# Two-step normalising at the start, att copies in older bursts, and one v product between two score tiles: a change to a group-norm attention kernel

## The chip, the cores and the metric

The kernel runs on one core of a Trainium2 chip. The metric is device time in microseconds: from the first to the last instruction of the core and what lies around them, as the median of several executions. The profile is of one further execution and lists every instruction with its engine, start and duration.

## What is computed

The input x has 4 batches of 512 channels by 48 x 48 pixels (T = 2304 positions). A batch is group-normalised (32 groups of 16 channels), projected to q, k and v, put through attention with 8 heads of 64 channels, projected again and added to x:

```
hn = _group_norm(x, gn_scale, gn_bias)
qkv = einsum('oc,bchw->bohw', qkv_w, hn) + qkv_b
q, k, v = (fp16, per head, d = 64)
w = softmax(einsum('bhct,bhcs->bhts', q * scale, k * scale), axis=-1)
a = einsum('bhts,bhcs->bhct', w, v).astype(float32)
out = einsum('oc,bchw->bohw', proj_w, a) + proj_b
return x + out
```

## The kernel before

The 512 channels lie in 4 chunks of 128 partitions (NC = 4), the 2304 positions in 5 blocks (NQ = 5): four of 512 columns and a last one, block 4, of 256. Heads are treated two at a time, as 4 pairs for each batch, so there are 16 pairs in all. `hn[b, c, j]` is batch b, chunk c, block j of x; it is normalised in place.

**Start.** Batch 0 is normalised before anything else can run. `stats` (L621) takes the statistics of one block on VectorE (DVE), `aggregate` (L625) joins the five of a chunk. For chunk 0, `first_group` (L678 to L686) averages over groups by two tiny matmuls with a matrix of sixteenths: one of the mean, then, after DVE has computed the variance with the deviation of the means (L680), one of that; GpSimd (POOL) raises to the power -1/2 (L686); DVE makes scale `ga` and bias `gb` (L690, L691); ScalarE (ACT) then applies them to the five blocks in the order 0 to 4 (`norm_chunk`, L706). Chunks 1 to 3 go through `group_scale` (L635 to L647) and `coefficients` (L654 to L666): a 32 x 32 transpose, `bn_aggr` over the 16 channels, the power on POOL, a copy that spreads the result, a transpose back, three small operations, and ACT again. DVE fits statistics of the next chunk between these steps. TensorE (PE) keeps its clock with matmuls on a constant (`keep_busy`, L1317) until it can begin the eight projection chains of pair 0 (L748): k of blocks 0 to 4, then q of blocks 0 to 2; all eight take chunk 0, then all take chunk 1, and so on.

**Stream.** Then comes a stream of bursts written out in program order. Burst n makes three score tiles (`scores`, L998: six matmuls of 512 columns, or twelve of 256 in block 4), whose exponentials ACT takes (L1005, tile by tile into `p`); three score banks rotate, so a tile waits for the exponential of the tile three before it. Two bursts later PE multiplies `p` with v (`values`, L1023, into the one bank `av`), and DVE copies a finished `av` to `avx` (L1032) and adds up `p` (`add`, L1054, L1059) for the softmax sums. The sums of a block are made by PE (`add_up`, L1082, into the same bank as `av`), copied to `slx` by DVE (L1098), sent through DRAM by SyncE (SP) and inverted (L1127); POOL divides (`divide`, L1147) and writes `att`. For blocks 2 and 3 of the last pair (`soon`; block 4 is the stream's end) the sums come two bursts after the block's end rather than three, and for block 3 DVE inverts in place (L1108).

**Work beside the stream.** All other work is a list of pieces. `fill` takes pieces from the list in each burst, as many as a credit allows: a projection of a later pair (L748, L799), or an output projection `pr` (L887, eight matmuls of 512 columns, evacuated by DVE at L914). `fill` runs after `values`, except in a burst that closes a block's sums, where it runs before. The output projection needs `att` as 32-bit copies `a32`, which `att32` makes on ACT (L881) or on POOL (L879). In the last batch the blocks 3, 2 and 4 are projected in two goes: pairs 0 to 2 first (FIRST, six matmuls; its three copies per block are issued together at the first of the block's pieces), pair 3 last (LAST, two matmuls).

The order on every engine is the program's order; each engine works its own list from front to back.

Of the kernel before, what the change touches and what calls it, by code (L numbers as in the profile page):

```python
# [24 lines left out]
GROUP = C // 32  # L25
# [442 lines left out]
def fast_path(  # L468
# [201 lines left out]
    def first_group():  # L670

        mean, var = moments[:, 1, 0:1], moments[:, 2, 0:1]
        by = share.rearrange("p g j -> p (g j)")
        pm = small_bank("first_group")
        dev, var2, mg, veps, rstd = (
            small_tile(1, f"first_{n}") for n in ("dev", "var2", "mg", "veps", "rstd")
        )
        nc.tensor.matmul(pm[:, 0:1], by, mean, start=True, stop=True)  # L678
        nc.vector.tensor_tensor(dev, mean, pm[:, 0:1], ALU.subtract)
        nc.vector.tensor_scalar(var2, dev, dev, var, ALU.mult, ALU.add)  # L680
        nc.tensor.matmul(pm[:, 1:2], by, var2, start=True, stop=True)
        nc.vector.scalar_tensor_tensor(
            mg, pm[:, 0:1], -1.0, gsc[:, 0:1], ALU.mult, ALU.mult
        )
        nc.vector.tensor_scalar(veps, pm[:, 1:2], EPS, None, ALU.add)
        nc.gpsimd.tensor_tensor(rstd, veps, mhalf[:, 0:1], ALU.pow)  # L686

        def finish():
            ga, gb = small_tile(1, "first_ga"), small_tile(1, "first_gb")
            nc.vector.tensor_tensor(ga, rstd, gsc[:, 0:1], ALU.mult)  # L690
            nc.vector.tensor_scalar(gb, rstd, mg, gbi[:, 0:1], ALU.mult, ALU.add)  # L691
            ab[0, 0] = ga, gb

        return finish
# [5 lines left out]

    def norm_chunk(b, c):

        ga, gb = ab[b, c]
        for j in range(NQ):
            t = hn[b, c, j]
            nc.scalar.activation(t, t, AF.Identity, bias=gb, scale=ga)  # L706

# [156 lines left out]
    def att32(b, j, pairs=range(NC)):  # L867
        o, n = QBLOCKS[j]
        for c in pairs:
            if left_over(b, j):  # L870
                t = xpool.tile([P, n], F32R, tag=f"x{c}_{j}", name=f"a32_{b}_{j}_{c}")
            else:
                t = work.tile(
                    [P, QB], F32R, tag=f"a32_{c}", bufs=1, name=f"a32_{b}_{j}_{c}"
                )
            at32[b, j, c] = t[:, :n]
            source = atts[b * NPAIR + c][:, o : o + n]
            if c in beside_exps() and not (pairs == LAST and left_over(b, j)):
                nc.gpsimd.tensor_copy(at32[b, j, c], source)  # L879
            else:  # L880
                nc.scalar.copy(at32[b, j, c], source)  # L881
# [55 lines left out]
    def proj_pieces(b, j):  # L937

        def ahead(k):
            if k < len(proj_list) and not in_two(b, proj_list[k][0]):
                residual(b, *proj_list[k])

        def begin():
            att32(b, j, LAST if in_two(b, j) else range(NC))
            if j == 0:
                ahead(0)
                ahead(1)

        pairs = LAST if in_two(b, j) else range(NC)
        chains = [
            proj_piece(b, j, chunks, pairs, lambda k=k: ahead(k + 2))
            for k, (jj, chunks) in enumerate(proj_list)
            if jj == j
        ]
        return [piece(0.0, begin)], chains
# [28 lines left out]
    def scores(u):  # L986
# [5 lines left out]
        for r in range(BURST):  # L992
            ps = ps_s.tile([P, 2, QB], F32, tag="ps", name=f"ps_{g}_{j}_{k}_{r}")
# [237 lines left out]
    def put_first(b, j):  # L1231

        for jj, chunks in proj_list:
            if jj == j:
                put([proj_piece(b, j, chunks, FIRST)])

    for b in range(B):
# [20 lines left out]
        if b == B - 1:  # L1258
# [4 lines left out]

            ahead = [
# [4 lines left out]
            ]  # L1269
            for j in range(NQ):  # L1270
                put_proj(old, j, ahead)
                if j + 1 < NQ:
                    put_convert(old, j + 1)

            for j in (NQ - 2, NQ - 3, NQ - 1):
                there = ends[(NG - 2) * NQ + j] + BEHIND + 6
                put_run(att32, b, j, FIRST, after=there)
                put_first(b, j)
# [34 lines left out]
    idle = ps_av.tile([P, QB], F32, tag="av", name="idle")  # L1313

    def keep_busy(count):
# [5 lines left out]
    def all_stats(c):  # L1321
        for j in range(NQ):
            stats(0, j, c)
        aggregate(0, (c,))

    keep_busy(16)
    all_stats(0)
    first_coefficients = first_group()
    keep_busy(4)

    eight = [(1, j) for j in range(NQ)] + [(0, j) for j in range(8 - NQ)]
# [10 lines left out]
    for c in range(NC):  # L1342

        for j in range(NQ):
            if j == (1 if c < 2 else 2):
                if c == 0:
                    first_coefficients()
                else:
                    coefficients(0, (c,))
                norm_chunk(0, c)  # L1350
            if c + 1 < NC:
                stats(0, j, c + 1)
        if c + 1 < NC:
            aggregate(0, (c + 1,))
            group_scale(0, (c + 1,))
# [75 lines left out]
    for n in range(end):  # L1431
# [5 lines left out]
        scores(stream[n])  # L1437
# [6 lines left out]
        if summed:  # L1444

            fill(n)
        if n >= BEHIND:
# [9 lines left out]
        if not summed:  # L1457
# [158 lines left out]
```

## Time and profile before

| What | us |
|---|---|
| median of 3 executions | 1601.38 |
| range of the three | 1600.72 to 1603.44 |
| the profiled execution, whole | 1602.89 |
| its span, first to last instruction | 1601.2 |
| PE busy | 1583.9 (99%) |
| ACT busy | 1268.1 (79%) |
| DVE busy | 1137.0 (71%) |
| POOL busy | 327.9 (20%) |

A timeline row gives the start in us from the span's start, the us up to the end of the merged group, the engine, the line of the kernel, the operation, out<-in with partitions and shape, the count, and in brackets the idle time before it with what ended it. PE's ends are modelled, so a busy PE can hide stretches in which it only waits; starts are measured, and the distance between the starts of the same step in two neighbouring bursts is the surer measure.

### The profile page before, as it was taken

The numbers are of one execution on the slowest core, as the hardware profiler recorded it, in microseconds if no ns is written. First come the engines' busy times: TensorE is split into PE (matmuls) and PEld (weight loads), VectorE is DVE, ScalarE is ACT, GpSimd is POOL, SyncE is SP. The second block draws the span as 40 slices with busy tenths as digits, with TensorE's granted clock in tenths as the row PEclk, the third lists the DMA queues.
The fourth block names the chain that finished last, engine by engine and source line by source line (L and its number), as shares of the span: only waits on it lengthen the run. The fifth ranks groups of instructions, "written<-read, shape, count | busy, mean of one in ns | idle before, by whom it ended". The sixth has DMA issues, their size and how long they took to land.

```text
span 1601.2 us, 28364 instructions
## 1 busy us (share of the span) xinstructions
PE 1583.9 (99%) x11524; PEld 695.0 (43%) x11524; DVE 1137.0 (71%) x1298; ACT 1268.1 (79%) x1362; POOL 327.9 (20%) x460
## 2 busy tenths in 40 slices
PE   9999999999999999999999999999999999999997
PEld 3533434443333534555333354445533334435554
DVE  6177668876666678887666666888767776766775
ACT  3177777888888888888888888877878888888895
POOL 1011212222121222222112111222212121111322
PEclk9999999999999999999999999999999999999999
DMA  7002020000000024521000001353101000015424
GB/s 217 8 14 67 11 71 17 18 15 12 14 18 15 9 70 119 145 64 28 11 15 18 14 12 41 111 154 90 25 15 18 15 15 11 15 31 163 151 67 128
DMA packets 94896, 82.10 MB, mean 51 GB/s; under 512 B 50852, under 2 KB 60964, under 8 KB 94756
## 3 DMA queue, kind: packets, MB, share of 16 engines
q1 hardware_dynamic: 92724, 78.35, 18.1%
q8 instruction: 92, 1.51, 0.4%
q10 hardware_dynamic: 1904, 1.84, 0.4%
q14 instruction: 48, 0.39, 0.1%
q0 software_dynamic: 128, 0.01, 0.0%
HBM read 60.70 MB, written 19.17 MB: 50 GB/s over the span
## 4 chain that ended last, share of the span: by engine, by line
PE 96%; DVE 1%; ACT 1%; DMA 1%; POOL 0%; issue 0%; SPq 0%; DVEq 0%
PE pqk L748 29%; PE ps L998 20%; PE av L1023 20%; PE pv L799 15%; PE pr L887 8%; PE sl L1082 2%; PE ps L748 1%; ACT p L1005 1%; DMA x<-x_dram 0%; DMA r<-x_dram 0%; DVE acc L1054 0%; PE first_av L748 0%; PE first_w L748 0%; DVE st L621 0%; POOL a L879 0%
## 5 line engine op out<-in xcount | busy, mean ns | idle before, releaser
L1005 ACT ACTIVATE p<-ps 128x1024 f16<-128x1024 f32 x1296 | 1233.3, 1025 | 302.5 <-PE ps L998 299.5
L1054 DVE TENSOR_TENSOR acc<-acc,p 128x3072 f16<-128x3072 f16 x270 | 487.2, 1805 | 54.0 <-ACT p L1005 51.6
L748 PE MATMUL pqk<-x,wqkv 128*64 128x512 f32 (+1 forms) x2432 | 510.2, 549 | 0.1
L1023 PE MATMUL av<-p,v 128*64 128x512 f16 (+1 forms) x2880 | 360.8, 364 | 0.4 <-DVE slx L1098 0.3
L998 PE MATMUL ps<-q,k 64*128 64x512 f16 (+1 forms) x2880 | 356.2, 358 | 1.5 <-ACT p L1005 1.1
L799 PE MATMUL pv<-wqkv,x 128*64 128x256 f32 x2304 | 267.5, 379 | 0.0
L748 PEld LDWEIGHTS pqk<-x,wqkv 128*64 128x64 f32 x2432 | 168.0, 137 | 205.9 <-issue 156.2
L1120 POOL TENSOR_SCALAR in<-sums 128x8 f32<-128x8 f32 (+1 forms) x158 | 101.3, 641 | 723.8 <-DMA sums<-slx 717.2
L998 PEld LDWEIGHTS <-k 64*128 64x128 f16 x2880 | 106.0, 94 | 288.5 <-issue 239.6
L1023 PEld LDWEIGHTS <-v 128*64 128x64 f16 x2880 | 131.3, 109 | 213.3 <-issue 168.6
L1147 POOL TENSOR_TENSOR att<-avx,ib 128x512 f16<-128x512 f32 (+1 forms) x78 | 126.5, 1622 | 434.2 <-DMA ib<-row 372.4
L799 PEld LDWEIGHTS pv<-wqkv,x 128*64 128x64 f32 x2304 | 161.7, 137 | 85.4
L1054 DVE TENSOR_TENSOR acc<-p,p 128x3072 f16<-128x3072 f16 x79 | 138.1, 1748 | 0.0
L887 PE MATMUL pr<-a,whi 128*128 128x512 f32 (+1 forms) x311 | 121.9, 399 | 2.6 <-DVE r L914 2.2
L1059 DVE TENSOR_TENSOR acc<-acc 128x1024 f16<-128x1024 f16 x156 | 112.5, 721 | 3.3
L887 PE MATMUL pr<-a,wlo 128*128 128x512 f32 (+1 forms) x311 | 113.6, 373 | 0.0
L758 DVE TENSOR_SCALAR k<-pqk,bqkv 128x512 f16<-128x512 f32 (+1 forms) x75 | 52.1, 695 | 77.4 <-PE pqk L748 77.2
L807 DVE TENSOR_TENSOR v<-pv,bv 128x512 f16<-128x512 f32 x72 | 49.6, 689 | 80.9 <-PE pv L799 80.8
L758 DVE TENSOR_SCALAR q<-pqk,bqkv 128x512 f16<-128x512 f32 (+1 forms) x77 | 53.4, 694 | 74.6 <-PE pqk L748 74.4
L1098 DVE COPY slx<-sl 128x512 f32<-128x512 f32 (+1 forms) x79 | 50.6, 640 | 66.0 <-PE sl L1082 66.0
L914 DVE SCALAR_TENSOR_TENSOR r<-pr,bproj,r 128x512 f32<-128x512 f32 (+1 forms) x80 | 54.9, 694 | 45.3 <-PE pr L887 40.2
L1032 DVE COPY avx<-av 128x512 f32<-128x512 f32 (+1 forms) x79 | 50.6, 640 | 38.5 <-PE av L1023 38.1
(102 smaller groups left out, 498.6 us busy)
## 6 DMA issues: line engine op xcount, KB each, us to landing
r<-x_dram SPq DMA_DIRECT2D x72, 256.0 KB, 3.6
out_dram<-r SPq DMA_DIRECT2D x69, 256.0 KB, 2.7
ib<-row SPq DMA_DIRECT2D x126, 128.0 KB, 3.1
x<-x_dram SPq DMA_DIRECT2D x62, 256.0 KB, 4.1
x<-x_dram SPq DMA_DIRECT2D x16, 128.0 KB, 5.0
sums<-slx SPq DMA_DIRECT2D x128, 2.0 KB, 2.1
ib<-row SPq DMA_DIRECT2D x30, 64.0 KB, 2.9
wqkv<-qkv_wT_dram SPq DMA_DIRECT2D x2, 768.0 KB, 6.9
```

Of the source, the lines that this page charges most:

```text
L748: nc.tensor.matmul(pw[0][lo : lo + D, :n], wqkv[:, c, w0 + lo : w0 + lo + D], hn[b, c, j], start=(c == 0), stop=(c == NC - 1),)
L758: nc.vector.tensor_scalar(qk[g][part][:, o : o + n], pw[0][:, :n], bqkv[:, col : col + 1], SCALE, ALU.add, ALU.mult,)
L799: nc.tensor.matmul(pw[0][lo : lo + D, a, :], hn[b, c, i * P // QB][:, at + lo : at + lo + D], wqkv[:, c, 2 * C + half * C // 2 :][:, : C / ...
L887: nc.tensor.matmul(ps[:, :n], w[:, c, bass.ts(m, P)], at32[b, j, c], start=(i == 0), stop=(i == len(steps) - 1),)
L914: nc.vector.scalar_tensor_tensor(xt[:, i], places[i], bias, xt[:, i], ALU.add, ALU.add)
L998: nc.tensor.matmul(ps[:, h, a * n : (a + 1) * n], kt[rows, bass.ts(i, P)], qt[rows, o : o + n], start=True, stop=True,)
L1005: nc.scalar.activation(pt[:, r], ps, AF.Exp)
L1023: nc.tensor.matmul(av[0][lo : lo + D, :n], vv[b, pr // 2][:, i, pr % 2 * P + lo : pr % 2 * P + lo + D], pt[:, r, h, a * n : (a + 1) * n], ...
L1054: nc.vector.tensor_tensor(t, before, pt, ALU.add)
L1059: nc.vector.tensor_tensor(t[:, 0], t[:, 0], t[:, r], ALU.add)
L1120: nc.gpsimd.tensor_scalar(t, sm, limit, None, op)
L1147: nc.gpsimd.tensor_tensor(atts[g][:, o : o + n], avx.pop((g, j))[:, :n], ibs.pop((g, j))[:, :n], ALU.mult,)
```

## The change

Three edits, each in its own place.

1. **Start.** Normalising is split in two steps where a block is needed first: ACT first applies the group-independent scale and the shift by the mean (`x * gsc + mg`, with mg = -mean * gsc), while the variance is still on its way; a second step multiplies by rstd and adds the bias. In chunk 0 block 4 and block 0 get this, block 4's second step by DVE and block 0's by ACT; in chunks 1 to 3 block 4 gets it, both steps by ACT. The variance of chunk 0's means is added by a second accumulating matmul, in a bank of its own. The eight chains now begin with k of block 4. DVE takes the statistics of chunk c + 1 before its coefficients and no longer between them; only block 0 of chunk 1 is still taken in between.
2. **Copies.** In the last batch, the copies of pairs 0 and 1 of the blocks 3, 2 and 4 are separate entries, one ahead of each of six output projections of batch 2, and remain on ACT; those of block 0 move from ACT to POOL. Pair 2's copy of block 3 goes ahead as well, and moves to POOL; those of blocks 2 and 4 are issued ahead of the first two projections of block 2. Block 2's early copies get tiles of their own that x has left (`x1_1`, `x3_1`).
3. **Near the end.** In the burst two after the end of the last pair's block 3, that block's last product with v stands between the second and third score tile. In the two bursts that follow the two `soon` sums, `fill` comes before `values`.

A listing of the two instruction orders shows besides that three projection pieces in the last batch's middle pairs move by half a chain, one burst earlier. SP's list is the same.

```
-        nc.tensor.matmul(pm[:, 0:1], by, mean, start=True, stop=True)
-        nc.vector.tensor_tensor(dev, mean, pm[:, 0:1], ALU.subtract)
-        nc.vector.tensor_scalar(var2, dev, dev, var, ALU.mult, ALU.add)
-        nc.tensor.matmul(pm[:, 1:2], by, var2, start=True, stop=True)
-        nc.vector.scalar_tensor_tensor(
-            mg, pm[:, 0:1], -1.0, gsc[:, 0:1], ALU.mult, ALU.mult
-        )
-        nc.vector.tensor_scalar(veps, pm[:, 1:2], EPS, None, ALU.add)
+        nc.tensor.matmul(pm, by, mean, start=True, stop=True)
+        nc.tensor.matmul(pv, by, var, start=True, stop=False)
+        nc.vector.tensor_tensor(dev, mean, pm, ALU.subtract)
+        nc.vector.tensor_tensor(dev2, dev, dev, ALU.mult)
+        nc.tensor.matmul(pv, by, dev2, start=False, stop=True)
+        mg = shifted(c, "a", pm)
+        small_first, then = hn[0, c, NQ - 1], hn[0, c, 0]
+        by_scalar(small_first, gsc[:, c : c + 1], mg)
+        by_scalar(then, gsc[:, c : c + 1], mg)
+        nc.vector.tensor_scalar(veps, pv, EPS, None, ALU.add)
         nc.gpsimd.tensor_tensor(rstd, veps, mhalf[:, 0:1], ALU.pow)
+        meanwhile()
+        by_vector(small_first, rstd, gbi[:, c : c + 1])
+        by_scalar(then, rstd, gbi[:, c : c + 1])
+        scale_bias(c, "a", rstd, mg)
+        for j in range(1, NQ - 1):
+            by_scalar(hn[0, c, j], *ab[0, c])
...
+    def next_group(c):
...
+        aggregate(0, (c,))
...
+        nc.vector.tensor_copy(by_group(means), to_channels(grouped[:, :, 0]))
+        nc.vector.transpose(mean_cols, means)
+        mg = shifted(c, tag, mean_cols[:, c : c + 1])
+        first = hn[0, c, NQ - 1]
+        by_scalar(first, gsc[:, c : c + 1], mg)
...
+        nc.vector.tensor_copy(by_group(scales), to_channels(rstd))
+        nc.vector.transpose(cols, scales)
+        by_scalar(first, cols[:, c : c + 1], gbi[:, c : c + 1])
+        scale_bias(c, tag, cols[:, c : c + 1], mg)
+        for j in range(NQ - 1):
+            by_scalar(hn[0, c, j], *ab[0, c])
...
-            if c in beside_exps() and not (pairs == LAST and left_over(b, j)):
+            if beside or c in beside_exps() and not (pairs == LAST and left_over(b, j)):
                 nc.gpsimd.tensor_copy(at32[b, j, c], source)
...
-            att32(b, j, LAST if in_two(b, j) else range(NC))
+            if in_two(b, j):
+                att32(b, j, LAST)
+            elif (b, j) == (B - 1, 0):
+                att32(b, j, range(len(EARLY), NC))
+            else:
+                att32(b, j)
...
         for r in range(BURST):
+            if r == BURST - 1 and ahead_of_last:
+                ahead_of_last()
...
+            ahead += [
+                (att32, b, j, (c,)) for j in (NQ - 2, NQ - 3, NQ - 1) for c in EARLY
+            ]
+            ahead.append((att32, b, NQ - 2, THIRD))
...
+            ahead = [
+                (att32, b, NQ - 3, THIRD),
+                (att32, b, NQ - 1, THIRD),
+                *((att32, b, 0, (c,), True) for c in EARLY),
+            ]
             for j in (NQ - 2, NQ - 3, NQ - 1):
-                there = ends[(NG - 2) * NQ + j] + BEHIND + 6
-                put_run(att32, b, j, FIRST, after=there)
-                put_first(b, j)
+                put_first(b, j, ahead if j != NQ - 2 else [])
...
-        scores(stream[n])
+        inside = n - BEHIND == soon[1]
+        scores(stream[n], (lambda: values(stream[n - BEHIND])) if inside else None)
...
-        if summed:
+        filled = summed or n - BEHIND - 1 in soon
+        if filled:
             fill(n)
-        if n >= BEHIND:
+        if n >= BEHIND and not inside:
             values(stream[n - BEHIND])
...
-        if not summed:
+        if not filled:
             fill(n)
```

## The prediction

> **What bounds the kernel now.** I read the busy times first, then PE's waits, then the timeline of the start and of the last 100 us, because the change touches only those.
>
> ```profile
> PE 1583.9 (99%) x11524; PEld 695.0 (43%) x11524; DVE 1137.0 (71%) x1298; ACT 1268.1 (79%) x1362; POOL 327.9 (20%) x460
> ```
>
> PE is the bound; what is not PE work can be won only where PE stands still. PE's waits, by what ended them:
>
> ```profile
> PE pr L887 <- DVE r L914: 2.2, 1, 2.2
> PE ps L748 <- ACT x L706: 1.3, 1, 1.3
> PE ps L998 <- ACT p L1005: 1.1, 3, 0.5
> PE av L1023 <- DVE slx L1098: 0.3, 1, 0.3
> PE sl L1082 <- DVE avx L1032: 0.2, 1, 0.2
> ```
>
> The first (near 1048 us, a late residual from DRAM) is not touched. The other four are what the edits can reach: the start, three waits for exponentials, one for `slx`, one for `avx`. The start, in the timeline:
>
> ```profile
> 9.07 0.38 PE L681 MATMUL first_group<-first_var,share 128*128 128x1 f32 x2 [0.56 <-DVE first_var L680]
> 9.80 0.58 POOL L686 TENSOR_TENSOR first_rstd<-first_veps,mhalf 128x1 f32<-128x1 f32 x1 [4.69 <-DVE first_veps L685]
> 10.49 0.27 DVE L691 TENSOR_SCALAR first_gb<-first_rstd,first_mg,gbi 128x1 f32<-128x1 f32 x1
> 10.80 3.42 ACT L706 ACTIVATE x<-x,first_gb,first_ga 128x512 f32<-128x512 f32 x5 [4.60 <-DVE first_gb L691]
> 11.67 4.94 PE L748 MATMUL ps<-x,wqkv 128*64 128x512 f32 x24 [1.34 <-ACT x L706]
> 18.16 4.89 PE L748 MATMUL ps<-x,wqkv 128*64 128x512 f32 x24
> ```
>
> Useful PE work starts at 11.67. A chunk takes 18.16 - 11.67 = 6.49 us and later ones 6.44 (24.60 - 18.16): a chain is 0.86 us for 512 columns, 0.43 for 256, and 7 x 0.86 + 0.43 = 6.45. So once begun PE doesn't stop, and the start is worth exactly what its first matmul gains, if it is then kept fed. The two stalls at the copies and the ones near the end, PE and ACT:
>
> ```profile
> 1512.73 1.67 ACT L881 CAST a<-att 128x512 fp32r<-128x512 f16 x3
> 1516.29 0.60 PE L998 MATMUL ps<-q,k 64*128 64x512 f16 x4
> 1517.20 0.39 PE L998 MATMUL ps<-q,k 64*128 64x512 f16 x2 [0.30 <-ACT p L1005]
> 1519.89 0.82 PE L998 MATMUL ps<-q,k 64*128 64x512 f16 x6
> 1530.45 0.39 PE L998 MATMUL ps<-q,k 64*128 64x512 f16 x2 [0.27 <-ACT p L1005]
> 1562.07 0.84 PE L1023 MATMUL av<-p,v 128*64 128x512 f16 x6 [0.35 <-DVE slx L1098]
> 1577.85 0.63 PE L998 MATMUL ps<-q,k 64*128 64x256 f16 x8
> 1579.00 0.39 PE L998 MATMUL ps<-q,k 64*128 64x256 f16 x4 [0.52 <-ACT p L1005]
> 1581.02 0.84 PE L1082 MATMUL sl<-acc,ones 128*64 128x512 f16 x6 [0.19 <-DVE avx L1032]
> 1582.43 0.83 PE L998 MATMUL ps<-q,k 64*128 64x256 f16 x12
> ```
>
> The bracket understates a stall, since a modelled end swallows part of it. Undisturbed bursts there with a six-matmul projection are 3.12 us apart by their score tiles (0.75 scores, 0.77 v product, 1.60 projection; 1523.34 to 1526.46). The burst at 1516.29 lasts 3.60, so its stall is 0.48, not 0.30; that at 1529.58 lasts 3.56 (to 1533.14): 0.44.
>
> **What the Trainium skill says.** "Perfetto Trace Analysis", section Identifying the Most-Contended Engine, says that matmul busy share is no good measure for TensorE because pipelined matmuls blur it. This trace agrees: 99% busy, with 0.48 us lost where 0.30 is shown; hence the distances. "ScalarE: Activation LUTs", Rules for kernel authors, gives about 0.3 us per activation and 0.83 ns per element: an estimate of 0.51 for 256 and 0.73 for 512; measured are 0.585 and 0.80 (0.71 from start to start), which I use. "GPSIMD Engine Reference", section 1 Specifications, has POOL share its memory interface with DVE. The trace agrees: a 512-column copy on POOL takes 0.61 alone and up to 2.23, DVE's 3072-column addition 1.75 and 2.06 to 2.12 beside POOL. It matters for the copies that go to POOL.
>
> **Edit 1, the start.** Removed from the path: the wait of the second matmul for DVE's 0.27 us variance (now a 0.15 us square: about 0.12 saved), `ga`, `gb` and the hand-over (10.38 to 10.80), and one ACT block of 512. New times: moments at 8.07; means at 8.51; dev 8.55, square 8.74 to 8.89; variance matmul 8.95 to 9.33; veps to 9.52; power on POOL 9.61 to 10.19. Meanwhile mg is ready at 9.09 and ACT shifts block 4 (9.13 to 9.71) and block 0 (to about 10.4). DVE's second step on block 4 has a like in the trace, the later `norm` of 256 columns, 0.36 us at least: 10.22 to 10.58, so PE starts at about 10.65 (a 0.07 hand-over as at 11.60 to 11.67). Its first chain lasts 0.43, to 11.08. Block 0 needs ACT's second step, 10.4 to 11.2: PE goes on at 11.25 and then has 7 x 0.86 = 6.02 to do, to 17.27 against 18.16: **0.9 us** gained; 1.05 if block 0 isn't late, 0.7 if ACT's two steps on one block follow each other 0.2 later.
>
> It must stay fed. DVE takes for a chunk about 2.75 (five statistics, four at 0.61 and one at 0.41) + 1.5 (aggregate to veps, 18.41 to 19.89) + 0.9 (POOL's power) + 0.95 (spread, transpose, ga, gb; 21.08 to 22.1, one small operation fewer) = 6.1 us, under PE's 6.45. Chunk 1's gb falls at about 16.25, since one statistics is already done and four follow from 10.8; ACT has block 0 some 0.9 later, 17.15, and PE wants it at 17.27 + 0.43 = 17.7: margin 0.5. With 6.1 against 6.45 it grows to 0.9 and 1.2 for chunks 2 and 3. Block 4 is ready before, by two ACT steps from 15.85. The added ACT steps (five) lie in ACT's idle time there (2.07, 2.42 and 1.52 us before each chunk); without that cover they cost 0.5 each. `keep_busy` still ends before 10.65.
>
> **Edit 2, copies.** Taken out of ACT's full bursts: 3 x 0.575 at 1512.73 and 2 x 0.575 at 1526.50, the 2 x 0.36 at 1539.41, and two of block 0 at 1546.0. The last two cost PE nothing that I can see (the burst at 1539.38 lasts 3.46, which is 3.12 and a 0.34 sum; the one at 1545.98 is 0.27 too long, but by POOL's copies, which remain), so I count nothing there. The first two were the stalls: **0.48 + 0.44 = 0.92**. Where they go: bursts with eight-matmul projections, 3.58 apart, in which ACT idles 0.68 to 0.80 after 2.86 of exponentials; a copy of 0.575 fits each. One place is tight: at 1490.50 two copies (1.15) of batch 2 stand already, and one more (0.575) comes right after and another a burst later. Exponentials that began at 1491.70 would end at 1495.13, and PE's third score tile, at 1495.37, needs them: 0.24 margin. I take nothing lost, 0.3 as the other end. POOL's new copies: block 3's third runs after 1506.5, wanted at 1515; block 0's two run after the division ending at 1533.3, wanted at 1547.5. POOL idles 4.4 to 10.4 us around them, so behind them nothing is late; beside DVE they may stretch an addition by 0.35, which DVE's idle time covers.
>
> **Edit 3, the end.** (a) `fill` before `values` after the first early sum: the wait for `slx` (1561.65 due, 1562.07 done) is filled with the projection, which waits for nothing: **0.42**. The probabilities are held 2.06 longer; their slot is next written at about 1564.9, the product ends at 1564.55: free. (b) From 1577.85 to 1582.43 is 4.58 us. The work is 0.75 scores, 0.77 product, 0.67 projection, 1.41 sums: 3.60. With the product after eight score matmuls, PE is at the third tile at 1577.85 + 0.50 + 0.77 = 1579.12, after its release at 1579.00; the product ends 1.0 earlier, so `avx` is copied by 1580.03 and the sums start at 1580.05 instead of 1581.02: **0.97**. ACT then is next: its six exponentials end at 1581.70, and the last burst's first tile is there at 1581.9, so ACT doesn't hold it. (c) The last burst's product waited 0.10 for `slx`; the projection goes first: **0.10**. From there to the end PE runs without a gap to 1588.1, and the parallel chain `slx`, inverse (3.35), division, copy, shifts by the same 0.97. The tail (inverse, att, copy, projections, stores, flag) hangs on both and moves along.
>
> **Sum.** 0.9 + 0.92 + 0.42 + 0.97 + 0.10 = 3.3 us, from 2.4 (0.7, 0.6, 0.35, 0.75, 0) to 3.6. Against the profiled execution's 1602.89 that gives 1599.6; that execution is 1.5 above the median of 1601.38, for which I forecast **1598.1**. The three pieces that move by half a chain are the same work on a full PE: nothing.
>
> **The rivals.** (A) As computed: 1598.1, own range 1597.2 to 1599.2. (B) The copies' stall moves to the older bursts: ACT at 1490 to 1496 is fuller than I think, or the first block-3 copy waits for its tile. For it: 0.24 margin. Against: each neighbour burst gives ACT 0.7 back. It takes back about the 0.92: 1599.0. (C) The untouched 2.2 us wait near 1048 is a DMA that took 6.9 us where the median issue lands in 3.6; a shifted phase can remove it. For: it occurs once. Against: its requests shift with PE. It gives 1595.9. (D) Slower: DVE's chain for chunks 1 to 3 is now strictly serial, with no statistics inside POOL's power. If a chunk takes 6.1 + e, PE waits for chunk 3 by 3e - 1.2 in all; from e = 0.4 it costs, from e = 1.5 it eats all 3.3, and at e = 2.6 it is 6.6, 1604.7. For: the margin at chunk 1 is only 0.5. Against: every step's duration is in the trace, and the loads are there by the time the statistics now come (19.88 before for chunk 3, 22.5 now).
>
> **How the numbers follow.** 0.2% is about what a measurement of this kernel can tell from no change: 3.2 us, so faster means under 1598.2, on top of my forecast. Chances: A 0.68, of which 0.44 under 1598.2 (the forecast lies under it, and the 0.27 near 1546, where ACT is relieved too, can only add) and 0.24 above; B 0.16, within; C 0.12, faster; D 0.04, slower. Faster 0.56, same 0.40, slower 0.04. The range leaves out C and D and the noise beyond the medians' own spread: 1596.4 to 1600.2.
>
> **What would show it.** Right: first projection matmul near 10.65 and chunk 1 from 17.2 to 17.3; no wait for ACT's x after it; bursts of 3.12 at about 1514 and 1527 throughout; no `slx` wait near 1561; 3.6 us between the two score starts before the end. Wrong: PE waits for ACT's x at chunk 1 to 3 (D), waits for p around 1490 (B), or a wait that replaces `slx`'s, such as exponentials waiting for a slot of p.

## The result and the profile after

| | before | after |
|---|---|---|
| median, us | 1601.45 (13 executions) | 1598.8 (13 executions) |
| lowest, us | 1600.72 | 1597.84 |
| profiled execution, whole / span, us | 1602.89 / 1601.2 | 1599.08 / 1597.4 |

The ratio is 0.998, 95% interval 0.9973 to 0.9988: 2.65 us by the medians. One execution of the kernel before took 1650 us and is left out of the ratio; without it that median is 1601.42. The forecast was 1598.1, range 1596.4 to 1600.2: the median lies 0.7 above it and inside the range. The larger chance (0.56) had gone to a median under 1598.2, and that did not come.

The busy times of the profile after:

```profile
PE 1583.3 (99%) x11526; PEld 695.1 (44%) x11526; DVE 1137.7 (71%) x1302; ACT 1269.4 (79%) x1363; POOL 331.0 (21%) x463
```

PE's busy time fell by 0.6 only: the work is the same, and what went were gaps. Four rows of its waits in the profile after (us in total, times, longest; the rows left out stand before the first useful matmul or at the flag, which is the last comparison of the kernel, on whose result every engine then branches):

```profile
PE ps L791 <- DVE x L687: 0.5, 1, 0.5
PE pr L936 <- POOL a L928: 0.4, 1, 0.4
PE pr L936 <- DVE r L963: 0.3, 1, 0.3
PE ps L1054 <- DVE v L850: 0.3, 1, 0.3
```

The waits for exponentials (1.1), for `slx` (0.3), for `avx` (0.2) and for ACT's `x` (1.3) are gone. What is left of the last one is 0.5 for the first block, now from DVE. The start of the kernel after, in its timeline:

```profile
9.00 1.30 ACT L684 ACTIVATE x<-x,mg_a,gsc 128x256 f32<-128x256 f32 x2 [0.88 <-DVE mg_a L678]
9.62 0.58 POOL L709 TENSOR_TENSOR first_rstd<-first_veps,mhalf 128x1 f32<-128x1 f32 x1 [4.51 <-DVE first_veps L708]
10.23 0.41 DVE L687 TENSOR_SCALAR x<-x,first_rstd,gbi 128x256 f32<-128x256 f32 x1
10.39 0.81 ACT L684 ACTIVATE x<-x,gbi,first_rstd 128x512 f32<-128x512 f32 x1
10.70 5.06 PE L791 MATMUL ps<-x,wqkv 128*64 128x256 f32 x24 [0.48 <-DVE x L687]
16.37 2.91 ACT L684 ACTIVATE x<-x,gb_b,ga_b 128x512 f32<-128x512 f32 x4
17.31 4.89 PE L791 MATMUL ps<-x,wqkv 128*64 128x256 f32 x24
```

PE begins at 10.70 (forecast 10.65) and comes to chunk 1 at 17.31 (17.27). Chunk 2 follows at 23.75 and chunk 3 at 30.19, 6.44 apart. The first chunk takes 6.61, because PE stops shortly for block 0; after that it never waits, and DVE's serial chain takes 5.97 for a chunk (its statistics begin at 16.07 and at 22.04). The copies, on ACT, in the older bursts:

```profile
1487.43 1.67 ACT L930 CAST a<-att 128x512 fp32r<-128x512 f16 x3
1488.98 2.87 ACT L1061 ACTIVATE p<-ps 128x1024 f16<-128x1024 f32 x3
1491.70 0.66 ACT L930 CAST a<-att 128x512 fp32r<-128x512 f16 x1
1492.29 2.86 ACT L1061 ACTIVATE p<-ps 128x1024 f16<-128x1024 f32 x3
1495.02 0.42 ACT L930 CAST a<-att 128x256 fp32r<-128x256 f16 x1
1495.82 2.85 ACT L1061 ACTIVATE p<-ps 128x1024 f16<-128x1024 f32 x3 [0.39 <-PE ps L1054]
```

For 8 us ACT has no gap between 1487.43 and 1495.43; then it waits for PE again (0.39). PE never waits for it there. The two bursts that held the stalls now last 3.12 each (by PE's score tiles: 1513.22 to 1516.34, and 1526.03 to 1529.15), and the stretch before the end reads:

```profile
1513.22 0.82 PE L1054 MATMUL ps<-q,k 64*128 64x512 f16 x6
...
1516.34 0.82 PE L1054 MATMUL ps<-q,k 64*128 64x512 f16 x6
...
1573.93 0.63 PE L1054 MATMUL ps<-q,k 64*128 64x256 f16 x8
1574.49 0.84 PE L1079 MATMUL av<-p,v 128*64 128x512 f16 x6
1575.26 0.39 PE L1054 MATMUL ps<-q,k 64*128 64x256 f16 x4
1575.58 0.50 PE L936 MATMUL pr<-a,whi 128*128 128x512 f32 x1
...
1576.25 0.84 PE L1138 MATMUL sl<-acc,ones 128*64 128x512 f16 x6
1576.92 0.81 PE L1138 MATMUL sl<-p,ones 128*64 128x512 f16 x6
1577.67 0.83 PE L1054 MATMUL ps<-q,k 64*128 64x256 f16 x12
```

From 1573.93 to 1577.67 is 3.74 us; before it was 4.58, and the forecast 3.60.

**Where the 3.8 us of the two profiles are.** Set against each other burst by burst (start of the first exponential of each burst, before minus after), the gain grows so:

| from | to | gain grows by | what |
|---|---|---|---|
| start | 1040 | 0.83 | edit 1 |
| 1040 | 1060 | 2.24 | the residual wait near 1048, in the profile of before only |
| 1510 | 1532 | 0.48 + 0.44 | the two stalls at the copies, edit 2 |
| 1533 | 1554 | -0.15, -0.33 | an addition of DVE that meets POOL's division; a residual that landed at 4.9 us for 4.3 |
| 1561 | 1565 | 0.41 | the `slx` wait, edit 3 |
| 1578 | 1583 | 0.84 | the product between two score tiles, edit 3 |
| 1583 | PE's last projections | 0.21 | the last burst's projection first, edit 3 |
| there | the flag | -0.19 | |
| flag | end | -0.97 | the tail, 6.36 before and 7.33 after |

The sum is 3.8. Two rows have nothing to do with an edit's plan: +2.24 near 1048 and -0.97 after the flag. The experiments ask what those are, and whether each edit alone gives its own part.

### The profile page after: what moved, and what is told of

It is laid out like the page before. It is cut to its first block, busy times and chain, and to the rows that moved or that the text cites. A ratio compares the mean times of both kernels' runs of the same rounds, so it can differ in the third digit from the quotient of the medians.

```text
span 1597.4 us, 28388 instructions
## 1 busy us (share of the span) xinstructions
PE 1583.3 (99%) x11526; PEld 695.1 (44%) x11526; DVE 1137.7 (71%) x1302; ACT 1269.4 (79%) x1363; POOL 331.0 (21%) x463
## 5 line engine op out<-in xcount | busy, mean ns | idle before, releaser
L1203 POOL TENSOR_TENSOR att<-avx,ib 128x512 f16<-128x512 f32 (+1 forms) x78 | 130.4, 1672 | 427.6 <-DMA ib<-row 372.6
```

What stands on the lines that cost most here:

```text
L1203: nc.gpsimd.tensor_tensor(atts[g][:, o : o + n], avx.pop((g, j))[:, :n], ibs.pop((g, j))[:, :n], ALU.mult,)
```

## The experiments

All kernels were timed in five rounds beside the kernel before on the same chip. The kernel before had there medians of 1601.97 (53 executions, with the first four), 1601.84 (48, the second four), 1601.66 (45, the next three) and 1601.45 (19, the last). I also compare means over all executions, with intervals by drawing executions again at random; the kernel after has then 39, in three runs. These means run over different chips; the kernel before alone has means from 1601.75 to 1602.10 on the four of them, so a difference of some 0.3 between two chips says little.

The first four were to show the parts. Where their texts speak of the tail or of PE's last branch: in the profile of before that branch takes 0.50 us, after 3.84, and one reading was that edit 1's additional PE entries lengthen the tail.

**Edit 1 alone.** The kernel before with the new `first_group`, `next_group` and order of the eight chains, and nothing else:

```
+        by_scalar(small_first, gsc[:, c : c + 1], mg)
+        by_scalar(then, gsc[:, c : c + 1], mg)
...
+        by_vector(small_first, rstd, gbi[:, c : c + 1])
+        by_scalar(then, rstd, gbi[:, c : c + 1])
```

> The change's edit 1 alone. Theory 1 (the parts add up, each worth what its stage shows): first projection matmul near 10.7, chunk 1 of PE near 17.3, no PE wait for x later, stalls at the copies and at the end as before; time 0.85 us less than before. Theory 2 (the start gains, but the end of the program gives it back: edit 1 adds an instruction to PE's list, and with it PE's last branch waits about 3.8 us for its instructions instead of 0.5): the branch takes about 3.8 here and the time is less by well under 0.85, or more than before. Theory 3 (that wait is luck of the single run): the branch's time is not tied to the edit.

Measured: median 1600.7 (21 executions), ratio 0.9991 (0.9985 to 0.9998), that is 1.4 us (0.3 to 2.4). First matmul at 10.55, exponentials 1.0 earlier all the way to 1040, and the wait near 1048 is 0.5 instead of 2.2. The executions lie within 1.6 us, those of before within 4.1. So this edit gives its 0.9, and seems to give something more.

**Edit 2 alone.**

```
+            if in_two(b, j):
+                att32(b, j, LAST)
...
-                put_run(att32, b, j, FIRST, after=there)
-                put_first(b, j)
+                put_first(b, j, ahead if j != NQ - 2 else [])
```

> Edit 2 alone. Theory 1: the bursts near 1516 and 1530 go back from 3.60 and 3.56 to 3.12 us; a new delay of 0.15 in the burst two later, where block 0's copies on POOL slow DVE's additions and so the release of the projection's bank; net 0.77 us less than before. Rival: the older bursts near 1490 lose as much as is won, 0.2 us or less in all. Theory 2: PE's last branch stays at 0.5 us, as PE's list keeps its length; theory 3: it may be either.

Measured: 1601.92 (13 executions), ratio 0.9997 (0.9988 to 1.0005). In the trace the gain grows by 0.93 over the two stalls (2.41 to 3.34), with nothing lost near 1490 and PE's waits for exponentials down from three to one. The timed interval, 0.8 slower to 1.9 faster, holds 0.92 and zero alike. The wait near 1048 is absent here, with an unchanged start: it comes and goes.

**Edit 3 alone.**

```
-        scores(stream[n])
+        inside = n - BEHIND == soon[1]
+        scores(stream[n], (lambda: values(stream[n - BEHIND])) if inside else None)
...
+        filled = summed or n - BEHIND - 1 in soon
```

> Edit 3 alone. Theory 1: the 0.42 wait for slx near 1562 goes, the last two score starts come 3.74 us apart instead of 4.58, and 0.1 to 0.2 more after them: 1.35 us less than before. Rival: the end is set by the stores and not by PE, and the time stays within 0.5 us of before. Theory 2: PE's last branch stays at 0.5 us; theory 3: it may be either.

Measured: 1601.49 (21 executions), ratio 0.9994 (0.9988 to 1.0001): 1.0 us, from 1.9 faster to 0.2 slower. In the trace +0.42 at `slx`, +0.87 at the product between the score tiles, +0.20 in the last burst: the profile's sum is 1.49. The tail is 7.69, the flag's gain 2.30, the span's 1.0.

**The change again.** The kernel after once more, beside these three:

> The changed kernel once more. Theory 2: PE's last branch takes 3.8 us again, since the program is the same. Theory 3: it differs. The projection's wait for a residual near 1048 us is absent as in the first profile if the phase decides it, and may come back if it is luck. Time 2.65 us less than before, 1 either way.

Measured: 1598.53 (9 executions), ratio 0.9975 (0.9965 to 0.9985). First matmul 10.61. The 0.33 at 1547 and the 0.15 at 1533 are not there; the addition of that burst is shorter (DVE in the kernel before; POOL and DVE in the kernel after; DVE in its repetition):

```profile
1533.92 1.75 DVE L1054 TENSOR_TENSOR acc<-acc,p 128x3072 f16<-128x3072 f16 x1
```

```profile
1529.32 1.28 POOL L1203 TENSOR_TENSOR att<-avx,ib 128x512 f16<-128x512 f32 x1 [3.62 <-ACT p L1061]
1530.54 3.16 POOL L928 CAST a<-att 128x512 fp32r<-128x512 f16 x2
1529.92 2.29 DVE L1110 TENSOR_TENSOR acc<-acc,p 128x3072 f16<-128x3072 f16 x1
```

```profile
1529.85 1.97 DVE L1110 TENSOR_TENSOR acc<-acc,p 128x3072 f16<-128x3072 f16 x1
```

The addition does not get longer by the two copies, which start inside it, but by POOL's division, which still runs when it starts: 0.67 us of it are left in the kernel after, and the addition takes 0.54 more; 0.36 are left in the repetition, and it takes 0.22 more. All 4886 additions of this size in the fourteen profiles agree: none takes over 1.8 us unless a POOL instruction is still running at its start, and the 1446 inside which one starts take at most 1.76.

The three parts' ratios multiply to 0.9982, 2.9 us; whole they were 0.998 and 0.9975. The parts add up within their intervals. PE's last branch took 0.50 in edit 3 alone and 3.25 in edit 2 alone, whose PE entries are as many as before's: edit 1 isn't what lengthens it.

**Is the wait near 1048 tied to edit 1?** The traces suggested a link, called P in what follows: the wait depends on where a fetch of PE's instructions falls. They are fetched in packets of 16 KB on a DMA queue of their own (92 in the page of the profile after). Edit 1 adds 4 PE entries, which moves one of these packets against SP's queue. Two kernels test it without any of the edits' work, by a longer and by a shorter chain of idle matmuls:

```
-    keep_busy(4)
+    keep_busy(6)
```

> The kernel before with nothing of the change; only the second of the two idle chains that keep PE's clock at the start is 6 matmuls long instead of 4, so that PE has 4 more entries (2 matmuls, 2 weight loads) that end before 11.67 and hide there. Theory P (the wait for the residual near 1048 us depends on where PE's 16 KB instruction fetch stands against SP's small DMAs): the fetch before burst 275 starts at 13.6 us or more ahead of its first exponential instead of 13.0, SP issues the broadcast of the inverse sums at about -11.6 instead of -10.7, the wait near 1048 is under 0.6 us instead of 2.2, first useful matmul stays at 11.5 to 11.7, and the median is 0.7 to 1.1 under the kernel before with a spread of its runs under 2 us. Theory S (it is edit 1's earlier start that moved that stage, or luck): the median is that of the kernel before within 0.3 us, and the spread stays 3 us or more.

```
-        keep_busy(4, ps_av.tile([P, QB], F32, tag="av", name="idle_again"))
+        keep_busy(2, ps_av.tile([P, QB], F32, tag="av", name="idle_again"))
```

> The kernel after with the second idle chain 2 matmuls long instead of 4, so that PE has 4 entries fewer from the start on; nothing else differs. Theory P: the fetch before burst 275 is back at about -13.0 us, SP's broadcast at -10.7, the wait near 1048 comes back in part of the executions, and the median is 0.7 to 1.1 us over the kernel after, about 1599.5, with a spread of 3 us. Theory S: same as the kernel after, 1598.5 to 1598.8, spread under 2 us. First useful matmul at 10.55 to 10.75 in both.

The first is on the kernel before, the second on the kernel after. SP's timeline in the kernel before, and then in the first of these two (the small DMA of the inverse sums, and the broadcast that waits for it, behind which the loads of the residual `r` stand in the queue):

```profile
1025.89 0.38 SPq L1129 DMA_DIRECT2D row<-inv  x1
1028.55 1.11 SPq L1139 DMA_DIRECT2D ib<-row  x2
1029.71 1.05 SPq L850 DMA_DIRECT2D r<-x_dram  x2
```

```profile
1025.67 0.38 SPq L1129 DMA_DIRECT2D row<-inv  x1
1027.59 1.11 SPq L1139 DMA_DIRECT2D ib<-row  x2
1028.76 1.05 SPq L850 DMA_DIRECT2D r<-x_dram  x2
```

Between the two issues lie 2.66 us and 1.92. In the kernel before, a window of the DMA view from 1026.2 to 1027.4 holds one packet of queue 8 and the small DMA's own:

```profile
q1 hardware_dynamic: 255, 0.00, 11.5%
q8 instruction: 1, 0.02, 5.8%
```

By the DMA records the fetch begins at 1026.30 and lasts 1.12 us. In the first test kernel it begins at 1025.36, before the small DMA. Taken back (the second test kernel), the interval is 3.10 (1024.92 to 1028.02). So P's first half is shown: those 4 entries move the fetch, and SP's broadcast and residual loads go out 0.7 and 1.4 later.

The times agree less well. Four entries added to the kernel before: 1601.43 (13 executions), ratio 0.9998 (0.9989 to 1.0006), 0.4 us where 0.7 to 1.1 was expected. Four taken from the kernel after: 1600.06 (21 executions), ratio 0.9989 (0.9982 to 0.9995); its mean is 1.43 (0.97 to 1.88) over that of the kernel after, over the 0.7 to 1.1 expected, though its interval takes in a part of that. The second result seems to need another cause beside P. And both kernels change one thing more than the fetch: PE idles 0.91 us before its first useful matmul in either, where the kernel before has 1.34 and the kernel after 0.48.

**Is it the two steps or the order?** The kernel before, with block 4 first but in one step:

```
-        for j in range(NQ):
+        for j in (NQ - 1, *range(NQ - 1)):
...
-    eight = [(1, j) for j in range(NQ)] + [(0, j) for j in range(8 - NQ)]
+    eight = [(1, j) for j in (NQ - 1, *range(NQ - 1))] + [(0, j) for j in range(8 - NQ)]
```

> The kernel before with one piece of edit 1 only: block 4 is normalised first and its chain comes first, in a single step from ga and gb as before; block 0 comes second. My account of edit 1: PE's first matmul comes about 0.2 us sooner (one ACT block of 256 takes 0.58 instead of 0.80: 11.45 for 11.67), but its chain lasts only 0.43, block 0 is ready 0.5 to 0.6 later than before, and all eight chains end at 18.1 to 18.2, as before: no gain, 1601 to 1602. So the 0.9 of edit 1 is the two steps' and not the order's. Rival: the order alone gives 0.2 or more at the second chunk (17.9 or less).

```profile
11.26 5.22 PE L748 MATMUL ps<-x,wqkv 128*64 128x256 f32 x24 [1.12 <-ACT x L706]
...
18.03 1.46 PE L748 MATMUL ps<-x,wqkv 128*64 128x256 f32 x8
```

PE starts 0.4 sooner than before and reaches chunk 1 only 0.13 sooner (18.03 for 18.16). Measured: 1602.06 (13 executions), ratio 1.0 (0.9992 to 1.0009), so anything from 1.3 faster to 1.4 slower. In the trace the order alone is worth 0.13; the rest of the 0.85 comes with the other parts of edit 1, the two steps above all (the variance's accumulating matmul was priced at 0.12).

**Does the end hang on the flag?** In the kernel after, POOL tests the last inverse sums before its last residual addition, and DVE reduces and compares earlier:

```
-    finish()()
...
     nc.gpsimd.tensor_copy(fines[:, n:], fine)
+    store_first = finish()
...
-        if i == NC:
+        if i == NC - 1:
```

> The kernel after, in which POOL tests the last block's inverse sums (four small operations) before its last residual addition instead of behind it, DVE reduces the result before the last two additions, and the flag comes between these two; that residual's store is issued last. By the rows of the profile after: tests from 1585.0 to 1587.7 instead of 1586.3 to 1588.9, reduction after DVE's four additions at 1587.9 instead of 1588.95, flag written at 1589.1 instead of 1590.03: 0.9 sooner. If the program's end hangs on the flag (7.3 us later), the time falls by 0.5 to 0.9, to about 1597.9; if it hangs on the last stores or on ACT's and DVE's last work (1589.8), by 0 to 0.3.

The flag's row in the kernel after and in this one (DVE):

```profile
1588.95 0.43 DVE L1615 TENSOR_REDUCE good<-fines 128x1 f32<-128x264 f32 x1 [0.49 <-POOL fines L1602]
1589.30 0.68 DVE L959 TENSOR_TENSOR r<-last_av,r 128x512 f32<-128x512 f32 x1
1589.89 0.13 DVE L1619 TENSOR_SCALAR flag<-count 1x1 int32<-1x1 f32 x1
```

```profile
1587.23 0.41 DVE L1615 TENSOR_REDUCE good<-fines 128x1 f32<-128x264 f32 x1
1588.17 0.14 DVE L1618 TENSOR_SCALAR flag<-count 1x1 int32<-1x1 f32 x1
1588.23 0.67 DVE L959 TENSOR_TENSOR r<-last_av,r 128x512 f32<-128x512 f32 x1
```

The flag falls 1.7 earlier, DVE's last work 1.1 earlier, the span's end 0.8 (1597.35 to 1596.54); beside the repetition of the kernel after, whose span is 1596.7, 0.2. Measured: 1598.33 (12 executions), ratio 0.9979 (0.997 to 0.9987); mean 0.24 under that of the kernel after (0.60 under to 0.14 over). The tail grew to 8.24: what comes after the flag took back most. This is the lowest median of all kernels here, and not one that can be told from the kernel after.

**More fetch positions.** Theory P as a window would let a fetch behind the small DMA be harmless too.

```
-    keep_busy(16)
+    keep_busy(12)
```

> The kernel before with the first idle chain 12 matmuls long instead of 16: 8 PE entries fewer, hidden before 7.9 us. The 4 entries of the earlier runs moved the instruction fetch before burst 275 by 0.7 us, so it should come 1.4 us later, at about -11.6 from that burst's first exponential, behind the small DMA of the inverse sums (issued at -13.4, landed by -11.6 where nothing is in its way). If only the meeting with that small DMA is the cost (theory P as a window): SP's broadcast goes out at -11.4 to -11.7, the standard deviation of the timed runs is under 0.85, and their mean is 0.4 to 1.4 us under the kernel before. If a fetch is better the earlier it comes, or the four entries act in another way (rival): the broadcast at -10.7 or later, deviation 0.95 or more, mean as before within 0.4. First useful matmul 11.4 to 11.7 in both.

The edit did something else. The clock column (the last but two) and PE's first chunk in this kernel:

```profile
0.00:10.00 10.00, 6.69 (x20) 2.47 (x20) 4.58 (x12) 1.28 (x1) 4.10 (x18) 1.00 0.87 260
10.00:20.00 10.00, 8.66 (x30) 2.71 (x30) 9.35 (x30) 6.84 (x10) 1.04 (x3) 0.66 1.06 379
20.00:30.00 10.00, 10.00 (x50) 3.37 (x48) 5.78 (x21) 6.41 (x10) 1.35 (x2) 1.00 0.45 152
```

```profile
11.60 7.92 PE L748 MATMUL ps<-x,wqkv 128*64 128x512 f32 x24 [1.34 <-ACT x L706]
...
21.07 1.45 PE L748 MATMUL ps<-x,wqkv 128*64 128x512 f32 x6
```

With 12 idle matmuls instead of 16 the granted clock falls to 0.66 between 10 and 20, and the first chunk takes 9.47 instead of 6.49: 2.98 lost. Measured: 1604.17 (21 executions), ratio 1.0015 (1.0008 to 1.0021). The fetch came at -12.86, not at -11.6, so the test of the window wasn't made. But it shows a second mechanism, K: the length of the idle chains can set the clock of the first chunk. By the trace's record of the clock, the full clock is granted at 7.39, half of it from 10.81 and the full clock again from 17.64, so the stretches last 3.42 and 6.83. PE does useful work for 6.04 of the 6.83; half of that is 3.02, against the 2.98 lost. "TensorE: Matmul & The Clock Gate", section Part 1: The HAM clock gate, of the Trainium skill says that the array runs at half clock until it has been busy for a window of some 3.4 us, and that these windows run freely, so that the point at which the clock changes differs from execution to execution. This trace agrees: its stretches are one and two such windows. And in the fourteen profiles the full clock is first granted anywhere from 4.37 to 7.39 us, where the idle matmuls change from 0.43 us apart to 0.22. One window at half clock would cost, as an estimate from the page's 3.4 us, half of it, 1.7 us.

```
-    keep_busy(4)
+    keep_busy(8)
```

> The kernel before with the second idle chain 8 matmuls long instead of 4: 8 PE entries more, ending at about 11.0, before the first useful matmul. The fetch should come at -14.3 to -14.5, well ahead of the small DMA. Theory P, either form: broadcast at -11.4 to -11.7, wait for the residual near 1048 under 0.6 us, deviation of the timed runs under 0.85, mean 0.4 to 1.4 us under the kernel before. Rival (chance): as the kernel before, deviation 0.95 or more.

Measured: 1601.34 (13 executions), ratio 0.9998 (0.999 to 1.0006); fetch at -14.81, broadcast at -11.68, no wait near 1048. With the other kernel that only adds idle matmuls, 26 executions, the mean is 0.45 (0.19 to 0.71) under that of 165 executions of the kernel before; beside their own chips the two are 0.38 and 0.39 under it. This gain isn't P's alone: the added matmuls also shorten PE's idle time, from 1.34 to 0.91 and 0.5.

> The kernel after with the first idle chain 12 matmuls long instead of 16: 8 PE entries fewer. Its fetch stands at -13.7 with all entries and at -12.9 with 4 fewer; with 8 fewer it should be at about -12.2, in which case the small DMA of the inverse sums, issued at -13.4, may still meet it. If the fetch lies behind that DMA's landing (-11.6 or later): broadcast at -11.4 to -11.7, deviation under 0.85, median as the kernel after, 1598.5 to 1598.8. If it still meets it: broadcast at -10.7 or later, deviation 0.95 or more, median 1599.5 to 1600.1.

This run has no edit in it: it is the kernel after once more, at 1598.52 (17 executions), ratio 0.998 (0.9972 to 0.9987), fetch at -13.70, broadcast at -11.64, wait near 1048 0.5. Its expectation isn't tested.

**P against K.** The last kernel takes the 4 entries from the kernel after, but keeps PE busy as long:

```
-        keep_busy(4, ps_av.tile([P, QB], F32, tag="av", name="idle_again"))
+        again = ps_av.tile([P, QB], F32, tag="av", name="idle_again")
+        nc.tensor.matmul(again, wide[:, :P], wide, start=True, stop=True)
```

> The kernel after in which the second idle chain of four 16-bit matmuls of 512 columns is one 32-bit matmul of 512 columns. In the profiles a 32-bit matmul is two entries of PE (the 128x1 rows of the start), so PE has 4 entries fewer, as in the run that put the fetch back, but it should stay busy for about 0.9 to 1.1 us there instead of 0.59, as in the kernel after. DVE fills 0.2 us more of constants at the start. Theory P (the place of the instruction fetch): as that run: fetch at -12.8 to -13.0, SP's broadcast at -10.3 to -10.7, mean 1599.8 to 1600.4, deviation 0.95 or more. Theory K (that run was slower because the shorter idle chain costs clock at the start in some executions): mean 1598.4 to 1598.9 as the kernel after, deviation under 0.85. First useful matmul at 10.5 to 10.75 in both; a 32-bit matmul of over 1.5 us would push it to 10.8.

```profile
8.96 1.10 PE L1396 MATMUL idle_again<-busy 128*128 128x512 f32 x2
10.47 2.06 PE L791 MATMUL ps<-x,wqkv 128*64 128x256 f32 x10 [0.40 <-DVE x L687]
```

```profile
1024.82 0.38 SPq L1185 DMA_DIRECT2D row<-inv  x1
1027.69 1.11 SPq L1195 DMA_DIRECT2D ib<-row  x2
...
1046.85 0.75 DVE L963 SCALAR_TENSOR_TENSOR r<-pr,bproj,r 128x512 f32<-128x512 f32 x1 [2.24 <-DMA r<-x_dram]
```

The idle time before PE's first useful matmul is 0.40, as in the kernel after (0.48), where the run with a shorter chain had 0.91. The broadcast waits 2.87, and DVE waits 2.24 for the residual: P's mark. Measured: 1599.16 (15 executions), ratio 0.9981 (0.9974 to 0.9989), mean 0.30 (-0.09 to 0.67) over the kernel after and 1.13 (0.61 to 1.65) under the run with the shorter chain. Neither theory has it whole. P is worth about 0.3 here, which can't be told from nothing, and not the 1.4; the other 1.1 goes with the shorter idle chain.

**All fourteen profiles together.** Times relative to the first exponential of burst 275; the wait is how much longer than 14.66 us the next four bursts take; the deviation is of the timed executions.

| kernel | fetch | broadcast | wait near 1048 | idle before first matmul | deviation |
|---|---|---|---|---|---|
| before | -12.99 | -10.74 | 2.2 | 1.34 | 1.0 |
| edit 2 alone | -12.84 | -10.73 | 0 | 1.3 | 0.96 |
| edit 3 alone | -13.04 | -10.73 | 1.2 | 1.3 | 1.03 |
| before, order only | -12.99 | -10.70 | 0.4 | 1.12 | 0.96 |
| before, 12 idle | -12.86 | -10.34 | 0.7 | 1.34 | 0.57 |
| after, 4 entries fewer | -12.86 | -10.30 | 0.8 | 0.91 | 0.99 |
| the same, kept busy | -12.58 | -10.52 | 1.2 | 0.40 | 0.67 |
| edit 1 alone | -13.63 | -11.57 | 0.6 | 0.5 | 0.46 |
| after | -13.73 | -11.67 | 0 | 0.48 | 0.81 |
| after, again | -13.93 | -11.59 | 0 | 0.5 | 0.38 |
| after, third | -13.70 | -11.64 | 0.5 | 0.48 | 0.51 |
| after, test first | -13.77 | -11.49 | 0 | 0.5 | 0.58 |
| before, 4 entries more | -13.71 | -11.47 | 0 | 0.91 | 0.66 |
| before, 8 entries more | -14.81 | -11.68 | 0 | 0.5 | 0.46 |

The broadcast follows the fetch without exception: seven late, seven early. The wait follows on average, 0.9 against 0.2. The deviation follows neither alone; it is near 1 where PE idles 0.9 or more and the fetch is late, but for the kernel with 12 idle matmuls, whose clock is low in all its executions (0.995 to 0.997).

## Why the prediction was right, point by point

**Edit 1, 0.9 forecast.** 0.83 by the exponentials and 0.85 at chunk 1 (18.16 to 17.31) in the first pair of profiles. Block 0 was late by the forecast amount: PE stops between block 4's chain and block 0's. DVE's `by_vector` took 0.41 where the nearest row gave 0.36, as much as lies between 10.65 and 10.70. That such small differences agree is luck: the old start begins PE at 11.48 to 11.67 in four profiles, the new one at 10.53 to 10.70 in the three of the kernel after. DVE's chunk took 5.97 for 6.1, and ACT's block 0 of chunk 1 was there at 17.18 against 17.74 wanted: margin 0.56 for 0.5. Rival D had no ground. The added ACT steps are four and not five (ACT has one instruction more, 1363, with three copies fewer); as they lie in idle time, nothing hangs on it.

**Edit 2, 0.92 forecast.** 0.48 and 0.44 in the trace, 0.93 alone; the timed runs can't tell this part from nothing. By the number alone, 1598.8 is nearer to rival B (1599.0) than to my 1598.1, but B's stall didn't come: after the copies at 1487, 1491 and 1495 ACT was still in time. The stretching of an addition, which I put at up to 0.35, was larger and had another cause: 0.54, by the division and not by the new copies, and the burst behind it lost 0.15, which I had said DVE's idle time covers. In the repetition it was 0.22 and nothing was lost; in edit 2 alone a copy still ran at the addition's start (0.41 left), and it was 0.27. I had read the stretched additions at 2.06 to 2.12; the profile of before has them up to 2.87, beside a division.

**Edit 3, 0.42 + 0.97 + 0.10 forecast.** 0.41, 0.84 and 0.21. The middle term was too large: the scores, cut in two by the product, take 0.56 (1573.93 to 1574.49) and 0.32 (1575.26 to 1575.58) where a burst in one piece takes 0.75, and so the stretch is 3.74 where the sum of the works gave 3.60. The last term was too small by 0.1. They sum to 1.46 for 1.49.

**What the forecast had not in it.** Three things of about the size of an edit, of both signs. First, the wait near 1048: I priced rival C at the whole 2.2 us, as if every execution had it. It varies from 0 to 2.2 with an unchanged start, so a change that removes it gains its mean, not what one profile shows. Edit 1's four PE entries do move the fetch that goes with it. In time that is worth about 0.3, perhaps nothing; the 0.4 of the kernels with entries only also holds their shorter idle time. "A shifted phase can remove it" was right in part, and "its requests shift with PE" was no argument against it, since the fetch moved with the number of PE entries and not with time. Second, the tail gave back 0.97 between these two profiles. Over the fourteen it lies between 6.4 and 8.2, and before's is the shortest, so that much of this may be that one profile; kernels with edit 3 have 7.2 to 8.2, those without 6.4 to 7.4. Third, the clock at the start may be a part of edit 1's gain: alone it gave 1.4 (0.3 to 2.4) for 0.9.

So 3.3 was forecast and 2.65, 3.4 and 3.1 were measured, and the terms of the sum stand each in the trace; but beside them the first pair of profiles has 2.24 of other gain and some 1.6 of other loss (0.15, 0.33, 0.19 and 0.97), which the prediction didn't see. That the timed gains came so close to the sum is in part luck.

**What stays open.** Whether K acts in the kernel before was not seen in a profile: but for the kernel with 12 idle matmuls, every profile has the full clock from PE's first useful matmul on. The timed executions list only a mean clock. On the first chip, 17 of 53 executions of the kernel before have 0.997 and a mean of 1603.07, and 36 have 0.998 and 1601.64; of edit 1 alone, 1 of 21 has 0.997. A window at half clock would fit the 1.4 between them. A longer tail would lower the mean too: in all fourteen profiles the granted clock is 0.5 from 1588.5 us or later to the end, which alone gives means from 0.9974 (the repetition of the kernel after) to 0.9985, but for the kernel with 12 idle matmuls (0.9962). So 0.997 by itself shows no low clock at the start. But what it costs differs. Over all chips 49 of the 165 executions of the kernel before have 0.997 or less and take 1.66 longer in the mean; that is 0.5 over all of them, as an estimate as much as edit 1 gained beyond its 0.9. In the kernels whose PE idles 0.5 or less, 15 of 100 have it, and it costs at most 0.5 but for one execution of the kernel after (0.996, 1601.06). This speaks for K in the kernel before and doesn't show it. What makes the tail long was not found, and with it 0.97 of the first pair of profiles stays unexplained: it doesn't go with PE's last branch (0.50 in tails of 6.36, 7.69 and 8.24; 3.84 in one of 7.33), and moving the flag moved the end little.

## What to carry to other kernels

Price a stall by the distance between the same steps of two undisturbed neighbours and name the next thing that is late; terms worked out so held here to about 0.15 us each, even where five such terms make 0.2% of a kernel. A wait that appears once in one profile has a distribution: look at other executions, or at kernels that differ elsewhere, before it is counted in full or left out in full. And an edit that adds or removes a few instructions moves everything that depends on their number, such as instruction fetches and how long an engine idles at the start; a control that has only the instructions, and none of the work, shows what part of the time is theirs, if it leaves the engine's idle time as it was.

## What the runs showed of the hardware that I had not expected

- An instruction fetch of PE (16 KB, 0.9 to 1.4 us) that starts beside a 4 KB DMA goes with a landing 0.7 to 1.4 later: 1.72 to 1.93 us from that DMA's issue to the next one's where the fetch is ahead, 2.66 to 3.10 where it falls beside it (seven profiles each).
- Four idle matmuls fewer at the start (12 for 16) cost 2.98 us in the first chunk: the clock is 0.5 from 10.81 to 17.64 us, although PE, once begun, had idled no longer than 1.24 us at a time before that.
- Behind the flag, every kernel takes 6.4 to 8.2 us to its end; a flag 1.7 us earlier ended the span 0.8 earlier, or 0.2 beside the repetition.
- A 3072-column addition of DVE gets longer where a POOL instruction still runs at its start (0.67 us left: 2.29 for 1.75; 0.36 left: 1.97). A POOL copy that starts inside the addition gets longer itself: two took 3.16 us, where one alone takes 0.61.
